# A graph-network stack on one core: units of the second convolution between the banks of the first, with rearranged loads, fill and comparisons

## The chip, the core and the metric

The kernel runs on one core of one Trainium2 chip. A core has a matrix engine (PE, with a record PEld for its weight loads), a vector engine (DVE), a scalar engine (ACT), a general engine (POOL) and a sync engine (SP). SP, ACT and POOL also issue DMAs, each in its own program order: an instruction that waits holds up all that stand behind it on the same engine. The metric is device microseconds of one execution.

## The reference, cut to what matters

Four graph layers follow each other on 3125 nodes and 50000 edges, each with a residual and a layer norm: three graph convolutions (L0), an attention layer (L1), an edge-gated layer (L2), ten graph convolutions (L3). The change touches only L0 and what prepares it.

```python
N, E, D = 3125, 50000, 128          # edges sorted by dst
def gcn_layer(x, src, dst, ew, W, b):
    s, d = concat(src, arange(N)), concat(dst, arange(N))
    w = concat(ew, ones(N))
    deg  = segment_sum(w, d);  dinv = rsqrt(deg)
    h = x @ W
    return segment_sum(h[s] * (dinv[s] * w * dinv[d])[:, None], d) + b
def L0(x):
    for W, b in ((W1, b1), (W2, b2), (W3, b3)):
        x = relu(gcn_layer(x, src, dst, ew, W, b))
    return x
x = layernorm(x + L0(x));  x = layernorm(x + L1(x));  x = layernorm(x + L2(x));  x = layernorm(x + L3(x))
```

With A the dense matrix of edge weights plus the identity, a convolution is relu(dinv · (A (dinv · x)) W + b). A is built once, in HBM, and read by all 13 convolutions.

## The kernel before, in words

**The matrix in HBM.** A has 25 row tiles of 128 source nodes and 7 **banks** of 464 destination columns (the last has 341). Two tables hold it, cut at bank `HALF` (L33): banks 0 to 3 and banks 4 to 6. `fill` (L105) makes a strip `eye` with an identity in a field of zeros (a memset of 6320 columns on POOL, L108) and writes it to each bank with one DMA on ACT (L112), bank 6 first: seven DMAs of 5.8 MB.

**The scatters.** Each edge's weight is then written to its place in A by 406 indirect DMAs on POOL (`SortedBuild.scatter`, L511, DMA at L518), 128 edges each. As edges are sorted by destination, they go in **passes** (`PASSES`, L30): (first stretch, last stretch, first bank, last bank, from which bank on all is complete). A stretch is 14 scatters. Before, pass 0 takes stretches 20 to 28 and completes banks 5 and 6; the next complete bank 4, bank 3, banks 2 and 1 together, and bank 0. A pass writes to one table, so it needs that table's fill.

**The front.** What a scatter writes, and where, is worked out on DVE by `prepare` (L398). `load` (L372) brings windows of `src`, `dst` and `ew` to SBUF on SP's queue, and `compare` (L412), for each edge, compares its key with those of 39 neighbours on each side: `same` (is_equal for both sides in one, 39 x (39 + C) elements, shift outermost), `more` (times the weights), `rest` (sum), `before` (max), and a dozen small operations, the last of which writes the index `at`. `degrees` (L480) then makes one-hot tiles `ohl`, `ohh`, `ohw` in 29 groups for 406 small matmuls that give `dinv`. `stretches` (L220) checks that the edges are sorted, from a tile `run` that it loads; its operations stand among the first on DVE. All this comes before, or beside, the scatters.

**The convolutions of L0.** `Convolutions.__call__` (L611) goes through the banks from 6 to 0. For a bank it multiplies 25 tiles of A, in five **pieces** of five tiles (`CK`; 1160 KB each, 852 KB for bank 6; piece 0 holds nodes 2560 and up, piece 4 nodes 0 to 639), with the rows `xs`, sums them in PSUM (`acc`, L626), copies that to `aggT`, and, seven matmuls into the next bank, multiplies by W (`po`, L638) and writes the rows of the next convolution (`done`). Nine pieces stay in SBUF for the three convolutions (piece 0 of every bank, piece 1 of banks 6 and 5: `adj`); all others are read anew into four buffers (`adj_k`), by DMAs on SP (L600). The first load of a bank waits for the last scatters of the pass that completes it (`after`, L528). SP's instructions stand in an order that the framework's scheduler has set when the program was built.

Of the kernel before, what the change touches and what calls it, by code (L numbers as in the profile page):

```python
# [13 lines left out]
OP = mybir.AluOpType  # L14
# [14 lines left out]

PASSES = ((20, 28, 4, 7, 5), (16, 20, 4, 5, 4), (12, 17, 0, 4, 3), (3, 12, 0, 3, 1), (0, 3, 0, 1, 0))  # L30
BELOW = ((20, 5), (16, 4), (12, 3), (3, 1))
FROM = ((17, 4),)
HALF = 4  # L33
BLOCKS = ((0, 4), (4, 4), (8, 3), (11, 3))
# [14 lines left out]
def tile_gnn_stack(ctx: ExitStack, tc: tile.TileContext, a: dict, out: bass.AP):  # L49
# [55 lines left out]
    def fill(pool, banks):  # L105
        wide = NP - P + NBK * BW
        eye = pool.tile([P, wide], F32, name="eye")
        nc.gpsimd.memset(eye, 0.0)  # L108
        nc.gpsimd.tensor_copy(eye[:, NP - P:NP], ident)
        for b in banks:  # L110
            v = eye[:, b * BW:b * BW + BW]
            nc.scalar.dma_start(bank(b), bass.AP(tensor=v.tensor, offset=v.offset,  # L112
                                                 ap=[v.ap[0], [P, NT], [1, BW]]))
# [106 lines left out]
    def stretches():  # L220
# [5 lines left out]
        with (  # L226
# [15 lines left out]
            run = one.tile([P, NCH + NEAR], I32, name="run")  # L242
            nc.vector.memset(run, NP)
            nc.sync.dma_start(run[:P - 1, :], bass.AP(
                tensor=dst.tensor, offset=dst.offset, ap=[[NCH, P - 1], [1, NCH + NEAR]]))
            nc.sync.dma_start(run[P - 1:, :NCH], bass.AP(
                tensor=dst.tensor, offset=dst.offset + (P - 1) * NCH, ap=[[NCH, 1], [1, NCH]]))
            bad = one.tile([P, 3 + len(BELOW + FROM)], F32, name="bad")
# [112 lines left out]
    class SortedBuild:  # L361
# [5 lines left out]
        def __init__(self, pool):  # L367
            self.at, self.total, self.ready, self.last = [], [], {}, []
            self.passes = list(enumerate(PASSES))
            self.st = [self.load(pool, 0)]  # L370

        def load(self, pool, q):  # L372

            W = NEAR - 1
            s0, s1, lo, hi, _ = PASSES[q]
            C, e0 = SC * (s1 - s0), SE * s0

            def window(v, name, left, none):
                t = pool.tile([P, left + C + W], v.dtype, name=f"{name}{q}")
                p0 = 1 if e0 < left else 0  # L380
                p1 = next(p for p in range(P, 0, -1) if e0 + p * C + W <= NCH * P)
                if p0 or p1 < P:
                    nc.vector.memset(t, none)
                nc.sync.dma_start(t[p0:p1], bass.AP(tensor=v.tensor, offset=v.offset + e0 + p0 * C - left,
                                                    ap=[[C, p1 - p0], [1, left + C + W]]))
                if p0:
                    nc.sync.dma_start(t[:1, left:], bass.AP(tensor=v.tensor, offset=v.offset + e0,
                                                            ap=[[C, 1], [1, C + W]]))
                for p in range(p1, P):
                    n = left + NCH * P - e0 - p * C  # L390
                    nc.sync.dma_start(t[p:p + 1, :n], bass.AP(
                        tensor=v.tensor, offset=v.offset + e0 + p * C - left, ap=[[C, 1], [1, n]]))
                return t

            return {"C": C, "e0": e0, "banks": (lo, hi), "src": window(a["src_r"], "src_w", W, -1),
                    "dst": window(a["dst_r"], "dst_w", W, 0), "ew": window(a["ew_r"], "ew_w", 0, 0.0)}

        def prepare(self, pool, scratch, ps):  # L398
            W, st = NEAR - 1, self.st
            st += [self.load(scratch, q) for q in range(1, len(PASSES))]  # L400
            pe_, ve = InOrder(nc.tensor), InOrder(nc.vector)
# [4 lines left out]

            def shifts(t, start, L):

                v = t[:, start:start + L]
                return bass.AP(tensor=v.tensor, offset=v.offset, ap=[v.ap[0], [1, W], [1, L]])  # L410

            def compare(q):  # L412
# [5 lines left out]
                both = ps.tile([P, 512], F32, name="both", bufs=2)  # L418
                ve.tensor_copy(both[:, :W + C], key[:, :W + C])
                ve.tensor_copy(both[:, 256:256 + C + W], t["ew"])  # L420
                same = scratch.tile([P, W, W + CM], BF16, name="same")
                ve.tensor_tensor(same[:, :, :W + C], shifts(key, 1, W + C),
                                 both[:, None, :W + C].to_broadcast([P, W, W + C]), op=OP.is_equal)
                more = scratch.tile([P, W, CM], F32, name="more")
                ve.tensor_tensor(more[:, :, :C], same[:, :, W:W + C], shifts(both, 257, C), op=OP.mult)
                rest = scratch.tile([P, C], F32, name=f"rest{q}")
                ve.tensor_reduce(rest, more[:, :, :C].rearrange("p k c -> p c k"), axis=AX.X, op=OP.add)

                before = scratch.tile([P, C], F32, name=f"before{q}")
                v = same[:, 0, W - 1:W - 1 + C]  # L430
                ve.tensor_reduce(before, bass.AP(tensor=v.tensor, offset=v.offset,
                                                 ap=[v.ap[0], [1, C], [W + CM - 1, W]]),
                                 axis=AX.X, op=OP.max)

# [45 lines left out]
            def degrees(q, g, first, last):  # L480
# [3 lines left out]
                                 t["lo"][:, c, None].to_broadcast([P, SC, P]), op=OP.is_equal)  # L484
                ohh = scratch.tile([P, SC, NT], BF16, name="ohh", bufs=2)
                ve.tensor_tensor(ohh, iota_ps[:, None, :NT].to_broadcast([P, SC, NT]),
# [49 lines left out]
    def tiles4(b):  # L536
        return 4 * b, min(NT, 4 * b + 4)
# [42 lines left out]
    class Convolutions:  # L580
# [25 lines left out]
        def finish(self):  # L606
            if self.late:
                self.late()
                self.late = None

        def __call__(self, xs, w, done):  # L611

            for b in reversed(range(NBK)):
                if self.built:
                    self.built.scatter(b)
                c0, c1 = b * BW, min(N, b * BW + BW)
                acc = self.ps.tile([P, 512], F32, name="acc", bufs=3)
                for n, t in enumerate(reversed(range(NT))):
                    if n % CK == 0:
                        j = n // CK  # L620
                        k = self.kept.get((b, j))
                        if k is None and (b, j) in self.keeps:
                            k = self.kept[b, j] = self.load(self.one, f"adj{b}_{j}", b, j)
                        if k is None:
                            k = self.load(self.stream, "adj_k", b, j)
                    nc.tensor.matmul(acc[:, :c1 - c0], xs[:, t, :], k[:, n % CK, :c1 - c0],  # L626
                                     start=(n == 0), stop=(n == NT - 1))
                    if n == LATE:
                        self.finish()
                if b % 2:  # L630
                    nc.vector.tensor_copy(self.aggT[:, c0:c1], acc[:, :c1 - c0])  # L631
                else:
                    nc.scalar.activation(self.aggT[:, c0:c1], acc[:, :c1 - c0], AF.Copy)  # L633

                def late(t0=-(-c0 // P), t1=-(-c1 // P)):
                    po = self.ps.tile([P, 4, D], F32, name="po", bufs=3)
                    for t in range(t0, t1):
                        nc.tensor.matmul(po[:, t - t0, :], self.aggT[:, t * P:(t + 1) * P], w,  # L638
                                         start=True, stop=True)
                    done(po[:, :t1 - t0, :], t0, t1)  # L640
                self.late = late

# [27 lines left out]
    def l0(built=None):  # L670
        with (
# [12 lines left out]
            for b in range(NB):  # L684
                scaled(conv.xs[0], x, *tiles4(b))
            for i in range(3):
                def done(sums, t0, t1, i=i):
                    v = rows.tile([P, 4, D], F32, name="v")[:, :t1 - t0, :]
                    times_dinv_plus(v, sums, bs[i], t0, t1)
                    if i < 2:  # L690
                        nc.vector.scalar_tensor_tensor(conv.xs[(i + 1) % 2][:, t0:t1, :], v, 0.0,
                                                       dinv_rows(t0, t1), op0=OP.max, op1=OP.mult)
                    else:
                        nc.vector.scalar_tensor_tensor(v, v, 0.0, x[:, t0:t1, :], op0=OP.max, op1=OP.add)
                        mv, rs = norm(rows, v, t1 - t0)
                        subtract_scale(x[:, t0:t1, :], v, mv, rs, t1 - t0)
                conv(conv.xs[i % 2], ws[i], done)
            conv.finish()
# [865 lines left out]
```

## Time and profile before

| what | value |
|---|---|
| time, median of 3 runs (lowest to highest) | 3528.95 us (3527.69 to 3528.95) |
| the profiled execution: its time, its span | 3527.32 us, 3525.3 us |
| busy: PE, DVE, POOL, ACT | 78%, 46%, 33%, 23% of the span |
| fill on ACT: first issue, last issue ends | 27.00 us, 125.8 us |
| scatters on POOL: first, last | 85.97 us, 611.65 us |
| first matmul of the first convolution of L0 | 286.39 us |
| a whole convolution with PE never waiting | 136.7 us |

A timeline line has start, duration, engine, line, operation, written<-read, count and, in brackets, the idle time before it with what ended it. A group line has busy time, mean ns of one, and idle time before it. A window line has the length of a stretch, busy time of each engine with its instructions, the granted PE clock, the mean share of the 16 DMA engines that was busy, and GB/s. `L168` is the line of a helper that keeps an engine's order, so tile names tell the operations apart.

### The profile page before, as it was taken

To read this page: it belongs to the slowest core of one execution; us is meant where nothing else is said; L and a number is where in the kernel's file an instruction comes from. 1 tells how busy PE (TensorE), PEld (TensorE's weight loads), DVE (VectorE), ACT (ScalarE), POOL (GpSimd) and SP (SyncE) were. 2 spreads that over 40 slices of the span, in tenths; PEclk is the share of its full clock that TensorE was granted. 3 is DMA by queue.
4 is the path that set the end of the run, shared out by engine and by line. 5 is a ranking of instruction groups with operands and counts; after the bars stand their busy time and mean duration, and the time that the engine had idled before them with its cause. 6 is when DMAs were issued, how large, how long until landed. Compare 5 with 4: busy or idle time off the path is not lost.

```text
span 3525.3 us, 33097 instructions
## 1 busy us (share of the span) xinstructions
PE 2749.9 (78%) x11379; PEld 1728.9 (49%) x11379; DVE 1628.6 (46%) x4412; ACT 795.1 (23%) x1248; POOL 1156.1 (33%) x1205
## 2 busy tenths in 40 slices
PE   0026204999668888757888878999999999999998
PEld 0023102555357777725666654555555555555554
DVE  7991000011437777747999985323232222233234
ACT  0000000000111111136777762111111112121111
POOL 1777777000067777506777750000000000000000
PEclk9999657999768888778999999999999999999999
DMA  7605204766434444346666658666766666666655
GB/s 275 234 1 194 68 0 141 241 214 235 128 99 103 105 107 105 82 119 202 203 202 202 203 162 302 216 222 195 232 202 210 223 201 217 221 199 214 218 196 190
DMA packets 442189, 623.77 MB, mean 177 GB/s; under 512 B 89975, under 2 KB 410027, under 8 KB 441995
## 3 DMA queue, kind: packets, MB, share of 16 engines
q1 hardware_dynamic: 363194, 499.91, 44.1%
q0 software_dynamic: 44352, 77.35, 8.4%
q10 hardware_dynamic: 34464, 44.31, 3.7%
q8 instruction: 91, 1.49, 0.2%
q14 instruction: 88, 0.71, 0.1%
HBM read 557.25 MB, written 64.38 MB: 176 GB/s over the span
## 4 chain that ended last, share of the span: by engine, by line
PE 50%; POOL 25%; issue 9%; DMA 7%; DVE 6%; ACT 2%; SPq 1%; ACTq 1%; DVEq 0%; POOLq 0%
PE acc L626 45%; POOL adj L518 11%; POOL xj L196 7%; POOL zj L196 6%; PE po L638 2%; PE sums L168 2%; DMA zj<-s_to_src,src_i 1%; DMA adj<-eye 1%; DMA xj<-s_right,src_o 1%; DVE msg L168 1%; DVE z L168 1%; ACT parts L925 1%; SPq L600 1%; DMA adj<-adj 1%; DMA s_left<-parts 1%
## 5 line engine op out<-in xcount | busy, mean ns | idle before, releaser
L626 PE MATMUL acc<-adj_k,xs 128*128 128x464 f32 (+1 forms) x3280 | 1261.9, 540 | 0.0
L626 PEld LDWEIGHTS acc<-adj_k,xs 128*128 128x128 f32 x3280 | 619.1, 190 | 593.8 <-issue 558.0
L626 PE MATMUL acc<-adj,xs 128*128 128x464 f32 (+1 forms) x1270 | 501.1, 541 | 222.2 <-DMA adj<-adj 222.2
L196 POOL DMA_INDIRECT xj<-s_right,src_o x392 | 374.0, 954 | 492.1 <-ACT parts L925 373.0
L518 POOL DMA_INDIRECT adj<-total,at x406 | 403.2, 993 | 201.5 <-issue 123.2
L626 PEld LDWEIGHTS acc<-adj,xs 128*128 128x128 f32 x1270 | 242.7, 194 | 440.3 <-DMA adj<-adj 211.5
L196 POOL DMA_INDIRECT zj<-s_to_src,src_i x392 | 371.7, 948 | 242.8 <-ACT parts L925 123.7
L648 DVE SCALAR_TENSOR_TENSOR v<-po,dinv,three 128x128 f32<-128x128 f32 x250 | 71.1, 344 | 589.4 <-PE po L638 589.4
L168 PE MATMUL pz<-w,eaT 128*128 128x256 f32 x784 | 243.3, 392 | 87.7 <-DVE msg L168 75.6
L168 PE MATMUL sums<-msg,of_edge 128*128 128x132 f32 (+1 forms) x1568 | 235.1, 319 | 15.3 <-DVE msg L168 15.3
L648 DVE SCALAR_TENSOR_TENSOR v<-po,dinv,b 128x128 f32<-128x128 f32 x75 | 21.3, 344 | 475.6 <-PE po L638 475.6
L168 PEld LDWEIGHTS sums<-msg,of_edge 128*128 128x128 f32 x1568 | 228.1, 232 | 16.4 <-DVE msg L168 16.0
L168 PE MATMUL zT<-ident,xj 128*128 128x128 f32 x784 | 144.4, 312 | 79.8 <-DMA xj<-s_right,src_o 79.2
L633 ACT ACTIVATE aggT<-acc 128x464 f32<-128x464 f32 (+1 forms) x52 | 27.6, 532 | 790.7 <-PE acc L626 790.7
L168 PE MATMUL deg_ps<-ohw,ohl 128*128 128x75 bf16 x406 | 30.3, 258 | 214.2 <-DVE ohw L168 214.2
L660 ACT ACTIVATE rs<-rs 128x4 f32<-128x4 f32 (+1 forms) x91 | 18.6, 205 | 784.1 <-DVE rs L659 778.5
L168 PE MATMUL pz<-td,of_node 128*128 128x256 bf16 x1176 | 193.3, 274 | 2.3 <-DVE of_node L168 2.3
L168 PEld LDWEIGHTS zT<-ident,xj 128*128 128x128 f32 x784 | 124.7, 213 | 111.5 <-DMA xj<-s_right,src_o 96.8
L168 PEld LDWEIGHTS pz<-w,eaT 128*128 128x128 f32 x784 | 118.8, 191 | 112.9 <-DVE msg L168 95.6
L631 DVE COPY aggT<-acc 128x464 f32<-128x464 f32 x39 | 25.0, 642 | 293.2 <-PE acc L626 293.2
L168 PEld LDWEIGHTS <-of_node 128*128 128x128 bf16 x1176 | 115.4, 98 | 64.2 <-DVE of_node L168 3.0
L168 ACT ACTIVATE leaky<-zT 128x512 f32<-128x512 f32 (+1 forms) x112 | 60.9, 543 | 373.0 <-PE zT L168 362.1
(182 smaller groups left out, 3107.7 us busy)
## 6 DMA issues: line engine op xcount, KB each, us to landing
adj_k<-adj SPq DMA_DIRECT2D x289, 1160.0 KB
adj<-eye ACTq DMA_DIRECT2D x7, 5800.0 KB
adj_k<-adj SPq DMA_DIRECT2D x39, 852.5 KB
adj<-adj SPq DMA_DIRECT2D x15, 1160.0 KB
eaT<-in_ea_t SPq DMA_DIRECT2D x56, 256.0 KB
drow<-s_local SPq DMA_DIRECT2D x28, 448.0 KB
eaT<-in_ea_t SPq DMA_DIRECT2D x56, 192.0 KB
drow<-s_local SPq DMA_DIRECT2D x56, 128.0 KB
```

The lines of the kernel that those rows point to most:

```text
L168: ins = getattr(self.engine, name)(*args, **kwargs)
L196: after_writers(nc.gpsimd.indirect_dma_start(out=to, out_offset=None, in_=table[:NP, :], in_offset=bass.IndirectOffsetOnAxis(ap=index[:, c ...
L518: s = nc.gpsimd.indirect_dma_start(out=table[:SPARE + (hi - b0) * NP * BW, :], out_offset=bass.IndirectOffsetOnAxis(ap=self.at[q][:, c:c + ...
L600: load = after_writers(nc.sync.dma_start(k[:, :, :w], bank(b)[:, j * CK:(j + 1) * CK, :w]), tables_adj[b >= HALF][0])
L626: nc.tensor.matmul(acc[:, :c1 - c0], xs[:, t, :], k[:, n % CK, :c1 - c0], start=(n == 0), stop=(n == NT - 1))
L631: nc.vector.tensor_copy(self.aggT[:, c0:c1], acc[:, :c1 - c0])
L633: nc.scalar.activation(self.aggT[:, c0:c1], acc[:, :c1 - c0], AF.Copy)
L638: nc.tensor.matmul(po[:, t - t0, :], self.aggT[:, t * P:(t + 1) * P], w, start=True, stop=True)
L648: nc.vector.scalar_tensor_tensor(to[:, t - t0, :], sums[:, t - t0, :], dinv[:, t:t + 1], bias, op0=OP.mult, op1=OP.add)
L660: nc.scalar.activation(rs[:, :n], rs[:, :n], AF.Sqrt)
L925: last = nc.scalar.activation(to[:, i], of, AF.Copy)
```

## The change

Five things change.

- **Passes and tables.** `HALF` becomes 5 (table 0: banks 0 to 4, table 1: banks 5 and 6), and there are six passes, again 406 scatters in all. Pass 0 writes to banks 5 and 6 alone. After 112, 182, 238, 294, 364 and 406 scatters there are complete: banks 6 and 5; 4; 3; 2; 1; 0.
- **Units ahead.** The first two convolutions of L0 are no longer one after the other. `AHEAD` lists units (convolution, bank, pieces): between two banks of the first convolution stand those parts of the second whose inputs are complete. A sum that lacks piece 4 goes to a new tile `part`, and the unit that brings piece 4 adds it. The third convolution is as before.
- **Loads.** A window is no longer loaded as 127 rows and one single row: 128 rows of the body, and, where the window leaves the array, a tail of 127 rows by 39 columns. Pass 0 is loaded on SP, the others on POOL. `run` is loaded in the same manner.
- **Fill.** The zeros of `eye` are written half by DVE, half by POOL.
- **Comparisons.** The neighbour runs innermost; the two sides have an operation each (`same` and `past`). `ohh` goes to PSUM as f32.

```diff
-PASSES = ((20, 28, 4, 7, 5), (16, 20, 4, 5, 4), (12, 17, 0, 4, 3), (3, 12, 0, 3, 1), (0, 3, 0, 1, 0))
-HALF = 4
+PASSES = ((20, 28, 5, 7, 5), (16, 21, 0, 5, 4), (12, 16, 0, 4, 3), (8, 12, 0, 3, 2), (3, 8, 0, 2, 1),
+          (0, 3, 0, 1, 0))
+HALF = 5
+AHEAD = ((0, 6, ALL), (0, 5, ALL), (0, 4, ALL), (1, 6, (0, 1)), (1, 5, (0, 1)), (1, 4, (0, 1)),
+         (0, 3, ALL), (1, 3, (0, 1)),
+         (0, 2, ALL), (1, 2, (0, 1, 2)), (1, 6, (2,)), (1, 5, (2,)), (1, 4, (2,)), (1, 3, (2,)),
+         (0, 1, ALL), (1, 1, (0, 1, 2, 3)), (1, 6, (3,)), (1, 5, (3,)), (1, 4, (3,)), (1, 3, (3,)), (1, 2, (3,)),
+         (0, 0, ALL), (1, 0, (0, 1, 2, 3)), (1, 6, (4,)), (1, 5, (4,)), (1, 4, (4,)), (1, 3, (4,)), (1, 2, (4,)),
+         (1, 1, (4,)), (1, 0, (4,)))
...
-        nc.gpsimd.memset(eye, 0.0)
+        nc.vector.memset(eye[:, :NP - P], 0.0)
+        nc.gpsimd.memset(eye[:, NP:], 0.0)
...
-            nc.sync.dma_start(run[:P - 1, :], bass.AP(
-                tensor=dst.tensor, offset=dst.offset, ap=[[NCH, P - 1], [1, NCH + NEAR]]))
+            nc.sync.dma_start(run[:, :NCH], bass.AP(
+                tensor=dst.tensor, offset=dst.offset, ap=[[NCH, P], [1, NCH]]))
+            nc.sync.dma_start(run[:P - 1, NCH:], bass.AP(
+                tensor=dst.tensor, offset=dst.offset + NCH, ap=[[NCH, P - 1], [1, NEAR]]))
...
-            st += [self.load(scratch, q) for q in range(1, len(PASSES))]
+            st += [self.load(scratch, q, nc.gpsimd) for q in range(1, len(PASSES))]
...
-                ve.tensor_tensor(same[:, :, :W + C], shifts(key, 1, W + C),
-                                 both[:, None, :W + C].to_broadcast([P, W, W + C]), op=OP.is_equal)
-                ve.tensor_tensor(more[:, :, :C], same[:, :, W:W + C], shifts(both, 257, C), op=OP.mult)
-                ve.tensor_reduce(rest, more[:, :, :C].rearrange("p k c -> p c k"), axis=AX.X, op=OP.add)
+                own_key = both[:, :C, None].to_broadcast([P, C, W])
+                ve.tensor_tensor(same, neighbours(key, W + 1, C), own_key, op=OP.is_equal)
+                ve.tensor_tensor(more, same, neighbours(both, 257, C), op=OP.mult)
+                ve.tensor_reduce(rest, more, axis=AX.X, op=OP.add)
+                ve.tensor_tensor(past, neighbours(key, 0, C), own_key, op=OP.is_equal)
+                ve.tensor_reduce(before, past, axis=AX.X, op=OP.max)
...
-                ohh = scratch.tile([P, SC, NT], BF16, name="ohh", bufs=2)
+                ohh = ps.tile([P, SC, NT], F32, name="ohh", bufs=2)
...
+        def sums(self, xs, b, pieces, w, done, part=None):
+            if self.built:
+                self.built.scatter(b)
+            c0, c1 = b * BW, min(N, b * BW + BW)
+            acc = self.ps.tile([P, 512], F32, name="acc", bufs=3)
+            tiles = [(j, q) for j in pieces for q in range(CK)]
+            late = LATE if len(pieces) == NT // CK else CK - 1
+            for n, (j, q) in enumerate(tiles):
+                if q == 0:
+                    k = self.piece(b, j)
+                nc.tensor.matmul(acc[:, :c1 - c0], xs[:, NT - 1 - j * CK - q, :], k[:, q, :c1 - c0],
+                                 start=(n == 0), stop=(n == len(tiles) - 1))
+                if n == late:
+                    self.finish()
+            whole = NT // CK - 1 in pieces
+            to = (self.aggT if whole else part)[:, c0:c1]
+            if 0 not in pieces:
+                nc.vector.tensor_add(to, acc[:, :c1 - c0], part[:, c0:c1])
...
+                for i, b, pieces in AHEAD:
+                    conv.sums(conv.xs[i], b, pieces, ws[i], dones[i], part)
+            for i in range(2 if built else 0, 3):
+                conv(conv.xs[i % 2], ws[i], dones[i])
```

Built, SP's loads for the two convolutions stand in this order. A bank's first load (written with its bank) waits for that bank's scatters; "(c, b, p)" is a load into one of the four buffers, for piece p of bank b in convolution c (0 the first, 1 the second).

```
bank 6, bank 5, bank 4 with their pieces
bank 3 p0 (waits for 238 scatters) | (1,4,1) (0,3,1) (0,3,2) (0,3,3)
bank 2 p0 (waits for 294)          | (0,3,4) (1,3,1) (0,2,1) (0,2,2)
bank 1 p0 (waits for 364)          | (0,2,3) (0,2,4) (1,2,1)
bank 0 p0 (waits for 406)          | (1,2,2) (1,6,2) (1,5,2) (1,4,2) (1,3,2) (0,1,1) (0,1,2) (0,1,3) (0,1,4) (1,1,1) ...
```

On PE the units stand in the order of `AHEAD`, but for (1,6,(0,1)) and (1,5,(0,1)), which mix. The loads and matmuls of L1, L2 and L3 stand as before.

More of the change, by code (lines that the diff above doesn't have):

```diff
@@ L27 @@
 SC = 14
-PASSES = ((20, 28, 4, 7, 5), (16, 20, 4, 5, 4), (12, 17, 0, 4, 3), (3, 12, 0, 3, 1), (0, 3, 0, 1, 0))
-BELOW = ((20, 5), (16, 4), (12, 3), (3, 1))
-FROM = ((17, 4),)
-HALF = 4
+PASSES = ((20, 28, 5, 7, 5), (16, 21, 0, 5, 4), (12, 16, 0, 4, 3), (8, 12, 0, 3, 2), (3, 8, 0, 2, 1),
+          (0, 3, 0, 1, 0))
+BELOW = ((20, 5), (16, 4), (12, 3), (8, 2), (3, 1))
+FROM = ((21, 5),)
+HALF = 5
+ALL = (0, 1, 2, 3, 4)
+AHEAD = ((0, 6, ALL), (0, 5, ALL), (0, 4, ALL), (1, 6, (0, 1)), (1, 5, (0, 1)), (1, 4, (0, 1)),
[4 more added lines that the diff above has]
+         (1, 1, (4,)), (1, 0, (4,)))
 BLOCKS = ((0, 4), (4, 4), (8, 3), (11, 3))
@@ L242, in stretches @@
             run = one.tile([P, NCH + NEAR], I32, name="run")
-            nc.vector.memset(run, NP)
-            nc.sync.dma_start(run[:P - 1, :], bass.AP(
-                tensor=dst.tensor, offset=dst.offset, ap=[[NCH, P - 1], [1, NCH + NEAR]]))
-            nc.sync.dma_start(run[P - 1:, :NCH], bass.AP(
-                tensor=dst.tensor, offset=dst.offset + (P - 1) * NCH, ap=[[NCH, 1], [1, NCH]]))
+            nc.vector.memset(run[:, NCH:], NP)
+            nc.sync.dma_start(run[:, :NCH], bass.AP(
+                tensor=dst.tensor, offset=dst.offset, ap=[[NCH, P], [1, NCH]]))
+            nc.sync.dma_start(run[:P - 1, NCH:], bass.AP(
+                tensor=dst.tensor, offset=dst.offset + NCH, ap=[[NCH, P - 1], [1, NEAR]]))
             bad = one.tile([P, 3 + len(BELOW + FROM)], F32, name="bad")
@@ L369, in __init__, with load @@
             self.passes = list(enumerate(PASSES))
-            self.st = [self.load(pool, 0)]
-        def load(self, pool, q):
+            self.st = [self.load(pool, 0, nc.sync)]
+        def load(self, pool, q, queue):
             W = NEAR - 1
@@ L379, in window, with part @@
                 t = pool.tile([P, left + C + W], v.dtype, name=f"{name}{q}")
[L380 to L392, printed above, removed]
+                n = left + C + W
+                def part(p0, p1, c0, c1):
+                    queue.dma_start(t[p0:p1, c0:c1], bass.AP(
+                        tensor=v.tensor, offset=v.offset + e0 + p0 * C - left + c0,
+                        ap=[[C, p1 - p0], [1, c1 - c0]]))
+                first, last = e0 < left, e0 + P * C + W > NCH * P
+                assert not (first and last) and W <= C
+                if first:
+                    nc.vector.memset(t[:, :left], none)
+                    part(0, P, left, n)
+                    part(1, P, 0, left)
+                elif last:
+                    nc.vector.memset(t[:, left + C:], none)
+                    part(0, P, 0, left + C)
+                    part(0, P - 1, left + C, n)
+                else:
+                    part(0, P, 0, n)
                 return t
@@ L405, in prepare, with neighbours @@
             CM = SC * max(s1 - s0 for s0, s1, _, _, _ in PASSES)
-            def shifts(t, start, L):
-                v = t[:, start:start + L]
-                return bass.AP(tensor=v.tensor, offset=v.offset, ap=[v.ap[0], [1, W], [1, L]])
+            def neighbours(t, start, C):
+                v = t[:, start:start + C]
+                return bass.AP(tensor=v.tensor, offset=v.offset, ap=[v.ap[0], [1, C], [1, W]])
             def compare(q):
@@ L418, in compare @@
                 both = ps.tile([P, 512], F32, name="both", bufs=2)
-                ve.tensor_copy(both[:, :W + C], key[:, :W + C])
+                ve.tensor_copy(both[:, :C], key[:, mid])
                 ve.tensor_copy(both[:, 256:256 + C + W], t["ew"])
-                same = scratch.tile([P, W, W + CM], BF16, name="same")
-                ve.tensor_tensor(same[:, :, :W + C], shifts(key, 1, W + C),
-                                 both[:, None, :W + C].to_broadcast([P, W, W + C]), op=OP.is_equal)
-                more = scratch.tile([P, W, CM], F32, name="more")
-                ve.tensor_tensor(more[:, :, :C], same[:, :, W:W + C], shifts(both, 257, C), op=OP.mult)
+                own_key = both[:, :C, None].to_broadcast([P, C, W])
+                same = scratch.tile([P, CM, W], BF16, name="same")[:, :C, :]
+                ve.tensor_tensor(same, neighbours(key, W + 1, C), own_key, op=OP.is_equal)
+                more = scratch.tile([P, CM, W], F32, name="more")[:, :C, :]
+                ve.tensor_tensor(more, same, neighbours(both, 257, C), op=OP.mult)
                 rest = scratch.tile([P, C], F32, name=f"rest{q}")
-                ve.tensor_reduce(rest, more[:, :, :C].rearrange("p k c -> p c k"), axis=AX.X, op=OP.add)
+                ve.tensor_reduce(rest, more, axis=AX.X, op=OP.add)
+                past = scratch.tile([P, CM, W], BF16, name="past")[:, :C, :]
+                ve.tensor_tensor(past, neighbours(key, 0, C), own_key, op=OP.is_equal)
                 before = scratch.tile([P, C], F32, name=f"before{q}")
[L430 to L433, printed above, removed]
+                ve.tensor_reduce(before, past, axis=AX.X, op=OP.max)
                 own = scratch.tile([P, C], F32, name=f"own{q}")
@@ L609, in finish, with piece @@
                 self.late = None
+        def piece(self, b, j):
+            k = self.kept.get((b, j))
+            if k is None and (b, j) in self.keeps:
+                k = self.kept[b, j] = self.load(self.one, f"adj{b}_{j}", b, j)
+            return self.load(self.stream, "adj_k", b, j) if k is None else k
+        def sums(self, xs, b, pieces, w, done, part=None):
[16 more added lines that the diff above has]
+                nc.vector.tensor_add(to, acc[:, :c1 - c0], part[:, c0:c1])
+            elif b % 2:
+                nc.vector.tensor_copy(to, acc[:, :c1 - c0])
+            else:
+                nc.scalar.activation(to, acc[:, :c1 - c0], AF.Copy)
+            if not whole:
+                return
+            def finish(t0=-(-c0 // P), t1=-(-c1 // P)):
+                po = self.ps.tile([P, 4, D], F32, name="po", bufs=3)
+                for t in range(t0, t1):
+                    nc.tensor.matmul(po[:, t - t0, :], self.aggT[:, t * P:(t + 1) * P], w,
+                                     start=True, stop=True)
+                done(po[:, :t1 - t0, :], t0, t1)
+            self.late = finish
@@ L611, in __call__ @@
         def __call__(self, xs, w, done):
             for b in reversed(range(NBK)):
[L614 to L640, printed above, removed]
@@ L641, in __call__ @@
-                self.late = late
+                self.sums(xs, b, range(NT // CK), w, done)
     def dinv_rows(t0, t1):
@@ L685, in l0 @@
                 scaled(conv.xs[0], x, *tiles4(b))
+            dones = []
             for i in range(3):
@@ L696, in done @@
                         subtract_scale(x[:, t0:t1, :], v, mv, rs, t1 - t0)
-                conv(conv.xs[i % 2], ws[i], done)
+                dones.append(done)
+            if built:
+                part = one.tile([P, NP], F32, name="part")
+                for i, b, pieces in AHEAD:
+                    conv.sums(conv.xs[i], b, pieces, ws[i], dones[i], part)
+            for i in range(2 if built else 0, 3):
+                conv(conv.xs[i % 2], ws[i], dones[i])
             conv.finish()
```

## The prediction

> **What bounds the kernel now.** I read the page's 40 slices first, then its groups, then the timeline of the first 800 us by engine. The convolutions of L0 should fill PE, but until slice 7 PE is mostly idle, while POOL is busy at seven tenths:
>
> ```profile
> PE   0026204999668888757888878999999999999998
> POOL 1777777000067777506777750000000000000000
> L518 POOL DMA_INDIRECT adj<-total,at x406 | 403.2, 993 | 201.5 <-issue 123.2
> ```
>
> Seven tenths is POOL at its rate: 0.96 us for a scatter and 0.30 us of issue. 406 of them take 406 x 1.263 = 513 us, more than all else there. What each waits for is in the timeline (POOL and ACT, then SP, then PE, around the start and the end of the scatters):
>
> ```profile
> 27.00 98.79 ACTq L112 DMA_DIRECT2D adj<-eye  x7
> 85.97 1.17 POOL L518 DMA_INDIRECT adj<-total,at  x1 [78.03 <-DMA adj<-eye]
> 163.29 1.99 POOL L518 DMA_INDIRECT adj<-total,at  x1 [0.30 <-issue]
> ...
> 611.65 0.96 POOL L518 DMA_INDIRECT adj<-total,at  x1 [0.31 <-issue]
> ...
> 614.00 0.36 SPq L600 DMA_DIRECT2D adj<-adj  x1
> ...
> 619.59 7.24 PE L626 MATMUL acc<-adj,xs 128*128 128x464 f32 x10 [10.66 <-DMA adj<-adj]
> ```
>
> The scatters start when the third bank's fill has landed (85.97) and end at 611.65. Bank 0's first load goes at 614.00, PE starts on it 5.6 us later and never waits again in L0. So the end is **the last scatter, plus the PE work then left**: bank 0 of the first convolution and all of the second and third. The first whole-bank steps of convolutions two and three in the chain start at 648.19 and 784.85, so a convolution is 136.7 us. From 614.00 to the third convolution: 5.6 + 3.2 (its first ten matmuls 7.24 instead of 4.05, at half the granted clock) + 20.4 (a bank) + 136.7 = 165.9 us. I work out the same two terms for the change. L1 to L3 do not change and shift by what L0 gains.
>
> **When the scatters start.** Two things must be there: two filled banks and pass 0's indices `at`.
>
> Fill. Its first DMA went at 27.00 though `eye` was ready at 7.5, since it waits (for a completion counter that it shares) for `run`. In the built new order it waits for the second load of the front, 127 short rows, and for `eye`, whose halves take 3100 x 0.85 ns (5.36 us for 6320 columns) = 2.6 us: issue near 5.6 us, first packets 0.9 us later. A bank's packets took 15.5 us (27.9 to 43.4); two take 31, the loads now beside them 4, and the engine that carries the tails is late by some 6 as before (bank 5: 15 engines at 63.3, the last at 68.9). **Two banks at about 48 us.**
>
> Indices. Loads of 127 rows are the catch. In this window of before, only they run, and one of 16 DMA engines is busy:
>
> ```profile
> 8.00:10.00 2.00, 0.00 (x0) 0.00 (x0) 0.00 (x0) 0.00 (x0) 0.00 (x0) 1.00 0.07 21
> ...
> 25.84 0.57 DVE L253 SCALAR_TENSOR_TENSOR scr<-run 128x392 f32<-128x392 int32 x1 [7.46 <-DMA run<-in_dst_r]
> 28.93 6.28 DVE L168 TENSOR_TENSOR same<-key,both 128x5889 bf16<-128x5889 f32 x1
> 39.98 8.28 DVE L168 TENSOR_REDUCE rest<-more 128x112 f32<-128x4368 f32 x1
> ```
>
> The tails are now 156 bytes a row, not 760, so alone one takes 127 x 14 ns = 1.8 us (packets of 4 bytes stand 9 ns apart, of 760 bytes 40). But the fill starts 21 us earlier and fills all engines; where 480-byte rows ran beside it (32 to 44 us) they stood 95 ns apart. At 90 ns, the two tails still to come, of `ew` and `run`, take 11.4 us each. From 6.7 us: two tails, 1.4 for `run`'s body, 0.9 to land, some 1 for POOL's loads in between: `run` at about 33, **7 us later than now**; with no contention 13. DVE stands still until then, since its first operation on `run` is ahead of all comparisons. From there to `same` is 3.1 us as now. Then `same`, `past`, `more` at 4368 x 1.07 ns = 4.7 us each, two reductions, and 4.0 us of small ones (56.46 to 60.93, less one step).
>
> Here a rule decides more than a row. The row has 8.28 us for a reduction of 4368 elements, 1.9 ns each; these lie 504 bytes apart. The Trainium skill (SBUF — State Buffer, Door 1: The DMA port swizzle) says that an access that crosses into a new 16-byte line each time pays a penalty and that neighbours don't. New, they lie side by side, so 4368 x 1.04 = 4.7 us. By the rule the indices are ready at 33 + 3.1 + 23.5 + 4.0 = 63.6, by the row at 71. I take the rule: operations of DVE that read side by side run at 1.04 to 1.07 ns an element throughout this trace. **The scatters start at 64 us** (bounds: 50, no contention; 76, more of it and the slow reductions), 22 earlier.
>
> POOL issues 17 loads before that, and its index iotas stand behind them. No row shows such a load; between nothing and an indirect DMA's 1.26 us each it is 0 to 21 us, so POOL is free by some 27 us, well before 64. At nothing, then; they would cost from 3.5 us each on.
>
> **How long the scatters take.** 15 of them last 1.5 to 2.0 us instead of 0.96, from 163 to 271 us, and every one starts within an `ohw`; 14.1 us together. The skill (SBUF — State Buffer, SBUF: two separate sides) has a DVE operation with two SBUF inputs, or in a two-port mode, keep POOL out for its whole length. By that, `xs<-x,dinv` at 276 to 283 would do so too, for 0.7 us each, but the scatter at 277.10 lasts 1.03. So I hold to the row: `ohw`, with all three operands bf16 in SBUF, blocks. Its input `ohh` is now f32 in PSUM, and the new comparisons have one operand in PSUM as the old ones, beside which no scatter was long. **14.1 us go**; kept, they stay (both ends). Last scatter: 64 + 405 x 1.263 = 575.7, **36 us earlier**, and bank 0's load near 578. The other fills end near 125 us, pass 1 begins at 205: hidden. `dinv` near 270 to 300 is hidden too: PE has all it can do before bank 3 done by some 373 us at either.
>
> **PE work left then.** The list of units promises much: with (0,3) to (1,2,(4)) done in the gaps, only bank 0 and 4 + 7 pieces of the second convolution would be left. But SP's order undoes most of it. Bank 0's first load, which waits for the last scatter, stands **ahead** of the loads for (1,2,2), (1,6,2) to (1,3,2) and all of (0,1) after its first piece, since the kept pieces have buffers of their own and were moved up; likewise (0,3,4) is behind bank 2's wait, (0,2,3) behind bank 1's. PE takes its units in order, so at the last scatter it stands within (1,2), and every piece from there is still to do: 32 pieces of 464 columns at 3.94 us (14.18 us for 36 of 10 records a piece) = 126.1, three of 341 at 2.92 = 8.8, eight `po` at 0.95 = 7.6, 3.1 for the clock, and 8.7 until the first can start (two loads must land: 5.6 + 3.1): **154.3 us against 165.9, 11.6 saved**. The 32 loads at 3.1 us each (pieces land at 566.4, 569.4, 572.5, 575.6) keep up, 99 us. The additions to `part` (0.65 us each on DVE) lie beside matmuls, with three `acc` buffers.
>
> **Sum.** 22 (start) + 14.1 (no blocked scatters) + 11.6 = 47.7 us. The profiled execution took 3527.3, 2.0 of it outside its span: 3479.6. The median of the runs is 1.6 higher: **3481 us**.
>
> **The rivals.**
> - *SP's order doesn't hold PE up*, so that units fill the gaps as listed. For it: the list. Against: the trace of before shows SP idle for 142.9 us at one such wait with nothing passing it. PE would be at bank 0 near 589, third convolution at 658 instead of 732: 3407.
> - *The front gains nothing*: tails and fill collide so that indices are ready only near 86. For it: 95 ns a row. Then 14.1 + 11.6 are left: 3503.
> - *POOL's queue becomes the bound, and it is slower.* The ninth and later loads wait for the first ones to land; if the queue's packets got through only as the fill ends (7 banks, 107 us, to near 120), iotas, indices and scatters follow at about 130. The gains of 25.7 are eaten from a start at 111.7 on, or loads of 6.3 us each on POOL; at 130 it is 3547. Against: while the fill ran (86 to 150 us) scatters kept their 1.26 us, and SP's rows got their turn.
>
> **How the numbers follow.** Forecast 0.81, the three rivals 0.05, 0.10 and 0.04. Start 50 to 76 is 3467 to 3493; blocked scatters kept add 14; pieces left, 5 either way: with the second rival 3463 to 3503. What a measurement can tell from no change is 0.2%, 7 us: 3522 to 3536. Faster 0.95, same 0.01, slower 0.04.
>
> **What would show it.** First fill issue at 5 to 7 us; `run` at DVE near 33; reductions of 4368 elements in 4.7 us; first scatter near 64; none of 2 us beside `ohw`; PE idle before (0,3)'s last piece and within (1,2) until bank 0's load; third convolution 154 us after that load. I am wrong if PE is seen on bank 1 before the last scatter, or if the first scatter is outside 50 to 76.

## The result, and the profile after

| | median of the runs, us | lowest to highest | profiled execution | its span |
|---|---|---|---|---|
| before | 3528.95 | 3527.69 to 3530.5 | 3527.3 | 3525.3 |
| after | 3481.4 | 3480.07 to 3483.56 | 3480.07 | 3478.3 |

After over before is 0.9866, with an interval of 0.9849 to 0.9883: 47 us less. The page of after has these lines for those first shown of before:

```profile
PE   0028334999588888658888869999999999999998
POOL 4777774000277777317777740000000000000000
L533 POOL DMA_INDIRECT adj<-total,at x406 | 395.9, 975 | 162.1 <-issue 122.6
```

POOL's first slice (of 87 us) is at four tenths instead of one, and its seventh at four instead of seven: the scatters start earlier and end earlier. They took 7.3 us less in all, though 14.1 us of stalls were to go from them: one that nothing holds up takes 0.972 us in the median, before 0.958. The timeline of the front (ACT's queue, DVE, POOL):

```profile
4.69 98.52 ACTq L123 DMA_DIRECT2D adj<-eye  x7
...
25.77 0.57 DVE L264 SCALAR_TENSOR_TENSOR scr<-run 128x392 f32<-128x392 int32 x1 [11.62 <-DMA run<-in_dst_r]
29.15 4.70 DVE L179 TENSOR_TENSOR same<-key,both 128x4368 bf16<-128x4368 f32 x1
38.63 4.70 DVE L179 TENSOR_REDUCE rest<-more 128x112 f32<-128x4368 f32 x1
...
56.90 1.05 POOL L533 DMA_INDIRECT adj<-total,at  x1 [38.59 <-DVE key L179]
```

The fill goes at 4.69, `run` reaches DVE at 25.77, a reduction takes 4.70 us and not 8.28, and the first scatter goes at 56.90 instead of 85.97. It waits for DVE, so for its indices, and no longer for the fill. No run puts the old comparisons back; in the two traces from the start of `same` to the end of pass 0's `at` is 32.1 us before and 27.5 after. Then PE and SP, from the gaps between the scatters to the third convolution:

```profile
434.41 0.36 SPq L615 DMA_DIRECT2D adj<-adj  x1
434.88 6.50 SPq L615 DMA_DIRECT2D adj_k<-adj  x4
443.51 6.68 PE L645 MATMUL acc<-adj_k,xs 128*128 128x464 f32 x10 [49.37 <-DMA adj_k<-adj]
...
533.28 10.07 PE L645 MATMUL acc<-adj_k,xs 128*128 128x464 f32 x20 [62.74 <-DMA adj_k<-adj]
...
577.68 0.36 SPq L615 DMA_DIRECT2D adj<-adj  x1
...
586.38 21.46 PE L645 MATMUL acc<-adj_k,xs 128*128 128x464 f32 x50 [34.58 <-DMA adj_k<-adj]
...
728.84 4.18 PE L645 MATMUL acc<-adj,xs 128*128 128x341 f32 x14
...
866.32 1.16 PE L663 MATMUL po<-w,aggT 128*128 128x128 f32 x8 [0.65 <-ACT aggT L656]
```

The last two of these steps, the start of the third convolution and the last `po` of L0, in the timeline of before:

```profile
779.78 4.18 PE L626 MATMUL acc<-adj,xs 128*128 128x341 f32 x14
...
917.32 1.16 PE L638 MATMUL po<-w,aggT 128*128 128x128 f32 x8 [0.71 <-ACT aggT L633]
```

After a first wait of 20.2 us at 371.94 (for (1,4,1), behind bank 3's wait), PE stands still for 49.4, 62.7 and 34.6 us, each time for a load of the second convolution or of a later piece (`adj_k`), not for a bank's first piece (`adj`). The load that the first of these three waits for, (0,3,4), is issued at 434.88, right behind bank 2's first piece, which had waited for the scatters until 434.41. Bank 0's first load goes at 577.68, PE works on from 586.38, and the third convolution starts at 728.84, 151.2 us after that load. The last `po` starts at 866.32 instead of 917.32: L0 gained 51.0 us, the span 47.0. The other 4.0 were given back after L0.

### The profile page after: what moved, and what is told of

The parts are those of the page before. It is cut to its first block, busy times and chain, and to the rows that moved or that the text cites. A ratio compares the mean times of both kernels' runs of the same rounds, so it can differ in the third digit from the quotient of the medians.

```text
span 3478.3 us, 33188 instructions
## 1 busy us (share of the span) xinstructions
PE 2759.6 (79%) x11379; PEld 1733.3 (50%) x11379; DVE 1630.3 (47%) x4476; ACT 795.5 (23%) x1248; POOL 1166.3 (34%) x1223
## 4 chain that ended last, share of the span: by engine, by line
PE 50%; POOL 25%; issue 9%; DMA 7%; DVE 6%; ACT 2%; SPq 1%; ACTq 0%; DVEq 0%; POOLq 0%
PE acc L645 45%; POOL adj L533 11%; POOL xj L207 8%; POOL zj L207 6%; PE po L663 2%; PE sums L179 2%; DMA zj<-s_to_src,src_i 2%; DMA ew_w<-in_ew_r 2%; DMA xj<-s_right,src_o 1%; DVE msg L179 1%; ACT parts L963 1%; DVE z L179 1%; SPq L615 1%; DMA s_left<-parts 1%; DVE h L965 1%
## 5 line engine op out<-in xcount | busy, mean ns | idle before, releaser
L645 PE MATMUL acc<-adj,xs 128*128 128x464 f32 (+1 forms) x1270 | 492.6, 534 | 14.2 <-DMA adj<-total,at 12.5
L533 POOL DMA_INDIRECT adj<-total,at x406 | 395.9, 975 | 162.1 <-issue 122.6
```

The source lines that it names most:

```text
L533: s = nc.gpsimd.indirect_dma_start(out=table[:SPARE + (hi - b0) * NP * BW, :], out_offset=bass.IndirectOffsetOnAxis(ap=self.at[q][:, c:c + ...
L645: nc.tensor.matmul(acc[:, :c1 - c0], xs[:, NT - 1 - j * CK - q, :], k[:, q, :c1 - c0], start=(n == 0), stop=(n == len(tiles) - 1))
```

## The experiments

There were twelve runs, of six variants of the changed kernel and of the kernel before. Four of them (e1b, e6, e2c, e7) ran on chips where the kernel before takes 3527 to 3531 us, as in the result; their times are compared with it. Where medians from different chips are compared, their ratios to the kernel before on each one's own chip give the same gain within 4 us. On the two chips of the others before takes 4236 and 4261 us: there `dinv` is not ready until after the last scatter (the last section shows the rows), so nothing of L0 can run beside scatters, and of these runs only the front and single DMAs are used.

### The order of the loads

```diff
+                if self.queued:
+                    follow(load, self.queued)
+                self.queued = load
```

This stands in `Convolutions.load`, where the tables are built: each load is made to follow the one asked for before it.

> The changed kernel, with SP's loads of the first convolutions held in the order in which the units use them. Theory (a bank's first load, moved ahead of older loads, holds them behind its wait for the scatters): PE has done all up to (1,2,(3,)) when bank 0's load comes near 577, goes on with bank 0 at 587 to 591 without a gap of 30 us, and reaches the third convolution near 656 instead of 728.8; about 3408 us. Rival (the units cannot run beside the scatters for another reason: contention of their loads, or inputs that come late): within 10 us of 3481.

> The loads of the units go to SP in the order in which the code asks for them (nothing else changes). Theory (SP's order held the units up: bank 0's load, which waits for the last scatter, stood ahead of the loads of (1,2) and (0,1)): PE works on the units between the scatters and is at bank 0 about 9 us after its load, with only bank 0 and the rest of the second convolution left. The third convolution starts near 656 instead of 729, and the time is 3408. Rival (PE has no room for the units before the last scatter, whatever the order): the third convolution stays near 729, time within 10 us of 3481.

e1_order (before 4260.59): 4237.66 us. PE did its first matmul of L0 at 709.70, after the last scatter, so this run tells nothing of either theory. e1b_order (before 3531.44): **3410.19 us** (3406.17 to 3412.84), ratio 0.9658, interval 0.9642 to 0.9675. Its timeline, PE and SP:

```profile
439.94 5.52 PE L648 MATMUL acc<-adj,xs 128*128 128x464 f32 x10 [40.06 <-DMA adj<-adj]
...
529.45 6.83 PE L648 MATMUL acc<-adj,xs 128*128 128x464 f32 x10 [41.55 <-DMA adj<-adj]
...
556.47 30.27 PE L648 MATMUL acc<-adj_k,xs 128*128 128x464 f32 x80
...
578.45 0.36 SPq L615 DMA_DIRECT2D adj<-adj  x1
...
586.58 4.05 PE L648 MATMUL acc<-adj,xs 128*128 128x464 f32 x10
...
653.40 4.18 PE L648 MATMUL acc<-adj,xs 128*128 128x341 f32 x14
```

The gaps are now waits for a bank's own first piece, so for scatters. At bank 0's load (578.45, within a microsecond of the changed kernel's) PE is in the middle of 80 matmuls of other units, and goes on to bank 0 at 586.58 without a gap. The third convolution starts 75.0 us after the load instead of 151.2. Against the changed kernel's median that is 71 us less. The theory's 3408 holds; the rival falls.

### Without the units

```diff
-                for i, b, pieces in AHEAD:
-                    conv.sums(conv.xs[i], b, pieces, ws[i], dones[i], part)
-            for i in range(2 if built else 0, 3):
+            for i in range(3):
```

> The changed kernel with the three convolutions one after the other; front, passes, fill and comparisons as changed. Theory (units ahead are worth only the difference of the PE work left after the last scatter, 151 us measured against 165.9): bank 0's load again near 577, third convolution near 743, 3493 to 3497 us. Rival (units ahead are what the change gains, the front little): 3515 or more.

> The three convolutions run one after the other as before, without the units; all else as in the changed kernel (four loads' depth, nine kept pieces, new front). Theory (of the 47 us the units bring only what was done of the second convolution before the last scatter, 11 to 15 us, since their loads stand behind bank 0's): third convolution near 743 instead of 729, time 3493 to 3497. Rival (the units bring most, the front little): third convolution near 765, time 3515 or more.

> The three convolutions one after the other as before, without the units; all else as in the changed kernel. On a chip where the kernel before takes 3530: theory (of the 47 us the units bring only what was done of the second convolution before the last scatter, 11 to 15 us): third convolution near 743 instead of 729, time 3493 to 3497. Rival (the units bring most, the front little): third convolution near 765, time 3515 or more.

e2_seq: 4239.29 beside 4260.59; e2b_seq: 4205.3 beside 4236.04; the first matmul of L0 at 709.71 and 708.16, so neither says what units bring. e2c_seq (before 3527.51): **3494.64 us** (3490.31 to 3496.63), ratio 0.9906, interval 0.9891 to 0.9921. Its timeline, SP and PE:

```profile
577.02 0.36 SPq L615 DMA_DIRECT2D adj<-adj  x1
...
740.96 4.18 PE L645 MATMUL acc<-adj,xs 128*128 128x341 f32 x14
```

From the load to the third convolution 163.9 us, where the changed kernel has 151.2: the units are worth 12.7 us in the trace and 13.2 in the medians. The new front, with all else, gives the other 33 by itself. The theory holds. Between this run and e1b_order lie 84 us (3494.6 and 3410.2): with their loads in order, the units bring several times what they bring as built. No run has the ordered loads without the units.

### The tails

A load of 127 rows is cut in two, 112 and 15 rows (the same for the windows of the passes):

```diff
-            nc.sync.dma_start(run[:P - 1, NCH:], bass.AP(
-                tensor=dst.tensor, offset=dst.offset + NCH, ap=[[NCH, P - 1], [1, NEAR]]))
+            for r0, r1 in ((0, 112), (112, P - 1)):
+                nc.sync.dma_start(run[r0:r1, NCH:], bass.AP(
+                    tensor=dst.tensor, offset=dst.offset + (r0 + 1) * NCH, ap=[[NCH, r1 - r0], [1, NEAR]]))
```

> The changed kernel with each tail of 127 rows loaded as 112 rows and 15 rows. Theory (127 rows go through one DMA engine and take turns with the fill there, 93.7 ns a row): run is there at 12 to 15 us instead of 25.8, indices near 44, the first scatter at 45 to 48 (then both fill and indices), 3469 to 3472 us. Rival (the wait for run is latency or issue, not the one engine): first scatter stays near 57, 3481.

> The tails of 127 rows cut into 112 and 15 rows, without the loads' order. Theory (the tail of run beside the fill holds DVE up, and the scatters' start sets the end): run at 12 to 15, first scatter near 46 instead of 57, time 3469 to 3472, the same gain as beside the loads in order (10 us). Rival (the start of the scatters no longer sets the end once SP's order holds PE up): first scatter near 46, time 3481.

> The loads in code order, and in addition the tails of 127 rows cut into 112 and 15 rows. Theory (the tail of run ran beside the fill as 127 packets of one engine, 94 ns each, and all comparisons stood behind it; split, its rows go over 16 engines): run is at DVE at 12 to 15, first scatter at 45 to 48 instead of 57, and the scatters, not PE, still set the end: 3397, 11 below the run with the order alone. Rival (PE's work, once it is in order, sets the end and not the last scatter): first scatter at 45 to 48 too, but no gain over the run with the order alone (3408).

The first scatter went at 45.61 in e4_tails (4226.88 us) and at 45.93 in e4b_tails (4196.4). On the same two chips the unsplit variants had it at 56.87 to 57.40, and their times were 4237.66 to 4243.18 and 4204.18 to 4205.3; there the scatters' end is what L0 starts on, so the expected 3469 to 3472 stays unmeasured. e6_both has the loads' order as well, and ran on one chip with e1b_order: **3400.2 us** (3399.68 to 3401.36), ratio 0.9629, interval 0.9613 to 0.9645, the fastest of all. Its timeline, DVE, POOL, SP and PE:

```profile
16.37 0.57 DVE L265 SCALAR_TENSOR_TENSOR scr<-run 128x392 f32<-128x392 int32 x1 [2.16 <-DMA run<-in_dst_r]
...
45.73 1.15 POOL L536 DMA_INDIRECT adj<-total,at  x1 [24.58 <-DVE at L179]
...
567.33 0.36 SPq L618 DMA_DIRECT2D adj<-adj  x1
...
641.78 4.18 PE L651 MATMUL acc<-adj,xs 128*128 128x341 f32 x14
```

Against e1b_order: first scatter 11.7 us earlier (57.41), bank 0's load 11.1, third convolution 11.6, median 10.0. The 127 rows of `run`'s tail pass from 13.94 to 15.67, in 1.7 us instead of 11.8. `run` is at DVE at 16.37, 1.4 us past the theory's 12 to 15, and the first scatter is where it was put; it still waits for the indices (45.4), not for the second bank's fill (41.0). So the scatters' start still sets the end when PE's work is in order: the rival falls.

### `ohh` back in SBUF

```diff
-                ohh = ps.tile([P, SC, NT], F32, name="ohh", bufs=2)
+                ohh = scratch.tile([P, SC, NT], BF16, name="ohh", bufs=2)
```

> The changed kernel with ohh in SBUF as bf16 again. Theory (ohw with all operands bf16 in SBUF keeps POOL out): some 15 scatters of 1.5 to 2.0 us come back beside ohw, the last scatter 14 us later, 3495 us. Rival (the long scatters came from something else in the old front): none comes back, 3481.

> ohh goes back to bf16 in SBUF, so that ohw has three bf16 operands in SBUF again; nothing else changes. Theory (such an ohw keeps POOL out for its length): 15 or so scatters of 1.5 to 2.0 us are back, the last scatter is 12 to 15 us later, and the end with it: 3493 to 3496. Rival (the long scatters came from something else of the change, or delay nothing): none of them is back, 3481.

e3_ohh took 4243.18 us and e3b_ohh 4204.18, both on the chips where time doesn't tell. The mechanism can be read there all the same. In the timeline of e3b_ohh, DVE and POOL:

```profile
220.62 1.25 DVE L179 TENSOR_TENSOR ohw<-ohh,three 128x1050 bf16<-128x1050 bf16 x1 [2.31 <-remote]
220.68 2.03 POOL L533 DMA_INDIRECT adj<-total,at  x1 [0.30 <-issue]
...
315.51 1.25 DVE L179 TENSOR_TENSOR ohw<-ohh,three 128x1050 bf16<-128x1050 bf16 x1
315.66 1.95 POOL L533 DMA_INDIRECT adj<-total,at  x1 [0.30 <-issue]
```

and in that of e4b_tails, on the same chip, with `ohh` in PSUM:

```profile
229.44 0.96 POOL L536 DMA_INDIRECT adj<-total,at  x1 [0.30 <-issue]
229.79 1.25 DVE L179 TENSOR_TENSOR ohw<-ohh,three 128x1050 bf16<-128x1050 f32 x1
230.71 0.96 POOL L536 DMA_INDIRECT adj<-total,at  x1 [0.30 <-issue]
```

The `ohw` lasts 1.25 us in both. Of the first five of each trace (up to 322 us), nine of ten with `ohh` in SBUF have a scatter of 1.21 to 2.03 us beside them; with `ohh` in PSUM none of 25 (e1_order, e2_seq, e4_tails, e2b_seq, e4b_tails) has one over 0.98. After 350 us scatters of 1.1 and some of 1.79 us stand beside both kinds on these chips, for a reason that I don't know, so that stretch isn't counted. The mechanism holds. What it is worth in time (the expected 12 to 15 us) was not measured by itself.

It is not only `ohw`. The changed kernel's trace has four scatters of 1.28 to 1.36 us left, and each begins within an `xs` multiply of DVE whose two inputs are f32 and both in SBUF. One of them, DVE and POOL:

```profile
300.26 0.56 DVE L721 SCALAR_TENSOR_TENSOR xs<-v,dinv 128x384 f32<-128x384 f32 x1
300.36 1.30 POOL L533 DMA_INDIRECT adj<-total,at  x1 [0.30 <-issue]
```

The scatter ends 0.84 us after that multiply. So do all eleven scatters of more than 1.2 us in the traces of the changed kernel, e1b_order, e2c_seq, e6_both and e7_loads_sp, each beside an `xs`, and the 15 beside `ohw` in the trace of before end 0.83 us after their `ohw`. Over these six traces, 139 scatters begin within a DVE operation with both inputs in SBUF and at least 0.035 us after its start; none ends sooner than 0.82 us after it. Of 647 that begin so within an operation with an input in PSUM, 260 end while it still runs. A scatter that begins in the last tenth of a microsecond of such an operation loses nothing, since it takes 0.97 us by itself.

### Why POOL's DMAs are slower

b2_before is the kernel before, once more; e7_loads_sp takes the loads of passes 1 to 5 from POOL's queue:

```diff
-            st += [self.load(scratch, q, nc.gpsimd) for q in range(1, len(PASSES))]
+            st += [self.load(scratch, q, nc.sync) for q in range(1, len(PASSES))]
```

> The kernel before as it is, once more with a profile, beside the changed kernel's variants. In the changed kernel's traces an indirect DMA of POOL took 0.96 to 0.97 us (zj 958 to 961 ns in the mean, 393 times), in the one trace of before 0.945 (zj 948). Theory (it differs by execution or chip): the mean of zj is 955 or more here too. Rival (the changed kernel makes POOL's indirect DMAs slower): zj is 948 again, scatters that are not held up 0.955.

> The 17 loads of passes 1 to 5 go to SP's queue as before, instead of POOL's. Question: why an indirect DMA of POOL takes longer in the changed kernel on the same chip (zj 956 to 961 ns in the mean against 948 to 949 before, scatters that nothing holds up 0.97 against 0.955 to 0.96). Theory (the loads on POOL's own queue make every later one slower): zj back at 948 to 950, scatters at 0.955 to 0.96, and the last scatter 5 us earlier if the front keeps its start. Rival (something else of the change does it): zj stays at 956 to 961.

b2_before took 4236.04 us on the chip of e2b_seq, e3b_ohh and e4b_tails. The groups of gathers on the pages of b2_before, then of e2b_seq:

```profile
L196 POOL DMA_INDIRECT zj<-s_to_src,src_i x392 | 372.0, 949 | 513.3 <-DVE z L168 243.3
```

```profile
L207 POOL DMA_INDIRECT zj<-s_to_src,src_i x392 | 375.8, 959 | 504.6 <-DVE z L179 225.7
```

949 ns before, 956 to 959 in the three variants on that chip: it goes with the kernel, not with the chip or the execution. e7_loads_sp took **3468.59 us** (3465.62 to 3470.12), ratio 0.9832, interval 0.9818 to 0.9845, but not for the reason that was tested. Its page and its timeline (DVE, ACT's queue, POOL):

```profile
L207 POOL DMA_INDIRECT zj<-s_to_src,src_i x392 | 375.5, 958 | 239.4 <-ACT parts L963 120.2
```

```profile
9.71 0.57 DVE L264 SCALAR_TENSOR_TENSOR scr<-run 128x392 f32<-128x392 int32 x1 [0.54 <-DMA run<-in_dst_r]
11.80 97.33 ACTq L123 DMA_DIRECT2D adj<-eye  x7
47.38 1.16 POOL L533 DMA_INDIRECT adj<-total,at  x1 [42.04 <-DMA adj<-eye]
```

The gathers stay at 958 ns: the loads on POOL's queue are not the cause, which is open. The time comes from the front. Here the fill starts 7.1 us later than in the changed kernel, so that `run` is through before it and at DVE at 9.71; the scatters then wait for the fill, and start 9.5 us earlier for it. It starts later because of a shared completion counter: in this trace ACT waits for the counter of `ew_w`'s tail, which a later load of `dst_w`, issued at 9.60, uses too; that one landed at 11.70. In the changed kernel it waits for the counter of `src_w`'s tail, which landed at 4.13. Bank 0's load goes at 567.33 and the third convolution starts at 718.75, 10.1 us before the changed kernel's. It is the gain of the split tails, got in another way.

## Why the prediction was right

The mechanism was the one forecast: the scatters start when the indices are ready and no longer with the fill, SP's order undoes most of the list, and the last scatter with the PE work then left sets the end. That 3481 meets the median of 3481.4 to half a microsecond is luck, since four terms were off and cancel:

| gain, us | forecast | measured |
|---|---|---|
| start of the scatters | 22 | 29.1 |
| their length | 14.1 | 7.2 |
| PE work left at bank 0's load | 11.6 | 14.6 |
| after L0 | 0 | -4.0 |
| in all | 47.7 | 47.0 |

- **The fill** was to go at 5 to 7 us and be through two banks at 48; it went at 4.69, and the packets of the second bank ended at 45.5.
- **`run` on DVE**, 33 us: it was 25.8. This term was mis-sized. I counted two tails of 127 rows beside the fill. The three tails of pass 0 were all through by 8.4 us, 15.7 ns a row, and only `run`'s went beside the fill, from 13.5 to 25.3 us, 93.7 ns a row. The price of such a row (90 ns) was right, their number was not; e6_both and e7_loads_sp take the one that is left away by splitting it or by moving the fill, and the scatters start 9.5 to 11.7 us earlier.
- **From `run` to the indices**, 30.6 us by the rule that elements side by side pay no penalty, 38 by the row of the old reduction. It was 30.8, with reductions of 4.70 us. The rule decided rightly; strides between 504 bytes and none were not run.
- **POOL's 17 loads**, bounded by 1.26 us each: most took 0.55, and POOL was free at 18.3. Hidden.
- **The blocked scatters** beside `ohw` are gone, and come back with `ohh` in SBUF. But my reading of the row at 277.10 was wrong. From its 1.03 us I held that `xs<-x,dinv` does not block; the `xs` beside it ran from 276.61 to 277.29, and the scatter ended 0.84 us after that, as every blocked one does. It had begun so late that it lost 0.07 us. The skill's wider rule, that two inputs in SBUF are enough, fits these traces, and mine, that all operands must be bf16, does not. The page has it only against a GpSimd operation that reads SBUF, a condition that I left out; a scatter takes its indices from a tile there. In time the slip is small: the four scatters held up by `xs` cost 1.4 us. What the stalls of `ohw` cost, 14.1 us, is from the trace of before alone.
- **405 x 1.263 us for the scatters** (511.5, so the sum is 575.5 and not 575.7): 518.5 us, or 1.280 each. The size was off by 7.0 us: 5.6 because an indirect DMA takes longer in the changed kernel, for a reason that stays open, and 1.4 for the four above. With the start 7.1 us early the last one came at 575.4.
- **What is left at bank 0's load**, 154.3 us: 151.2. The 8.7 until PE can start was exact (577.68 to 586.38), and the clock cost 2.9 us, forecast 3.1 (the first ten matmul records took 6.75 us, ten later ones 3.89). A piece took 3.89 instead of 3.94, and the eight `po` 6.5 instead of 7.6.
- **SP's order undoes most of the list**: three gaps of PE stand where they were put, within (0,3), within (0,2) and within (1,2). The rival in which the order does not hold PE up was given 3407; made true by e1b_order it takes 3410.2.
- **L1 to L3 only shift**: they gave 4.0 us back. From the last `po` to the end before has 2608.0 us, after 2612.0, e1b 2613.5, e2c 2614.3, e7 2612.1, e6 2618.7. In L1 POOL's gathers `xj` take 498.1 us from the first to the last, before 492.2, in L2 `zj` 494.7 after 489.8. These 10.8 us of slower DMAs are a term that was missing; 6.8 of them come back in the stretches around the gathers, and why e6 takes 5 to 7 us more than the others is open.

With the rivals: the front did gain (first scatter 29 us earlier), and POOL's queue was no bound.

## What to carry to other kernels

A list of work in a clever order is worth only what the in-order queue that feeds it lets through: read each queue as built, look for the first entry that waits long, and count what stands behind it that could already go (here one chain of three lines was worth 71 us, more than the whole change). A few short rows on one DMA engine are cheap alone (10.6 to 15.7 ns each here) and dear beside a stream that fills all engines (93.7), so either send them before the stream starts or cut them so that they go over more engines (1.7 us instead of 11.8 for the 127 rows in e6_both). When a row seems to refute a rule, look at where in the other operation it begins: a scatter that starts late in a blocking one shows almost nothing of it. And when a forecast lands on the median, compare its terms all the same: two errors of 7 us hid behind one sum.

## What the runs showed of the hardware that was not expected

On two chips the kernel before took 4236 and 4261 us instead of 3529, at nearly the same granted clock in the mean (0.897 against 0.917 in the profiles). In the timeline of b2_before while scatters run, DVE and PE:

```profile
320.85 2.02 DVE L168 TENSOR_TENSOR ohl<-iota_b,lo_f 128x1792 bf16<-128x1792 f32 x1 [35.46 <-remote]
...
324.64 1.04 PE L168 MATMUL deg_ps<-ohw,ohl 128*128 128x75 bf16 x14 [38.16 <-DVE ohw L168]
```

Each piece of `degrees` comes 39.2 us after the last one, though its operations take the 2.0 and 1.25 us they take elsewhere; the wait is one that the profile has no releaser for ("remote", "issue"), and it ends with the scatters: from 655 us on a piece takes 3.65. L1 and L2, where gathers run, are longer on these chips too (`xj` from the first to the last 669.7 us instead of 492.2 in the kernel before). The cause was not found.

Two more: the 127 rows of `run`'s tail, 160 bytes each, stood 10.6 ns apart ahead of the fill (e7_loads_sp, where from 8.10 to 8.70 us 0.08 of the 16 DMA engines was busy, little more than one of them) and 93.7 beside it; and POOL's gathers `zj` took 956 to 961 ns in the mean in every trace of the changed kernel and its variants, 948 and 949 in the two traces of before, wherever the loads went.
